# Transforms along w as 64x64 quarters; the second spectral layer by groups of 192 channels

## The chip, the cores and the metric

The kernel runs on one core of a Trainium2 chip. The metric is the device time of one execution in microseconds (us); lower is better. A core has a matrix engine (TensorE, PE in the profile, with PEld for its weight loads), VectorE (DVE), ScalarE (ACT), GpSimd (POOL) and the sync engine (SP), which here only issues transfers. Transfers are issued from SP's and ACT's queues. Matmul results land in PSUM[...] and are copied from there to SBUF by DVE or ACT. Everything is 32-bit floating point.

## The reference

Four layers work on an image of 48 x 48 positions with 768 channels. Layer 0 is a transformer block (attention, then an MLP with gelu), layer 2 a recurrent scan of twelve steps. Layers 1 and 3 are the same spectral block with different weights, and they are what the change is about:

```python
xs = jnp.fft.rfft2(xf32, axes=(1, 2))          # along h and w; 25 frequencies along w
xs = xs.reshape(B, H, Wm, NUM_HEADS, BLOCK)    # 8 blocks of 96 channels
o1r = relu(xr @ w1[0] - xi @ w1[1] + b1[0])    # per block of channels
o1i = relu(xi @ w1[0] + xr @ w1[1] + b1[1])
o2r = o1r @ w2[0] - o1i @ w2[1] + b2[0]
o2i = o1i @ w2[0] + o1r @ w2[1] + b2[1]
out_c = softshrink(o2r) + 1j * softshrink(o2i)
out = jnp.fft.irfft2(out_c, s=(H, W), axes=(1, 2))
return out + x
```

All transforms are matrix products with small constant matrices.

## The kernel before

The stages follow one another: layer 0's projections, attention, the output projection, the MLP, the first spectral layer (names beginning with f1), the scan, the scan's output product (so), and the second spectral layer (f3). A profile line L1529 is line 1529 of the kernel.

A spectral layer has five steps. Forward along w: `spectrum_rows` (L1529) takes a group g of four pairs of image rows and a half of the channels (384). A pair fills 96 partitions, two rows of 48 positions, and one matmul with `fw` of 96 x 112 (both rows' transforms in one matrix, half of it zeros) gives 112 rows of PSUM; ACT and DVE take turns in copying them out (`Evac`), and SP stores the four to `yu` in DRAM. There are 12 such blocks per layer: two halves, six groups. The first layer's run beside the MLP: `afno_follow` gives out one block at a time, `follow` is called between the MLP's matmuls, and its results take the two PSUM buffers of the pool `pt`. The MLP's own products use the pool `pm` with six. The second layer's run beside the scan's output product, whose results `x3` stay in SBUF.

Then `spectrum_mix` goes over items: a half, a group kc of five frequencies, a block b of 96 channels; 2 x 5 x 4 = 40 items. Four stages work on an item: transform along h (`s_fft_h`, L1593), the two layers of the small MLP (`s_mlp1`, L1607 to L1609; `s_mlp2`, L1628 and L1629, then softshrink as `cl` and `Z` on DVE), and the way back along h (`s_ifft_h`, L1643). A step of the loop runs the last stage on item step-4, the third on step-3, the second on step-1, the first on step, then calls `beside(step)`. The finished values of a half and kc (`us`) are stored to `yu` (L1652). In the first layer `us` has the layer's input in the frequency domain added to it (L1646); in the second it is a plain copy by ACT and DVE in turn.

Last comes the way back along w. In the first layer it is `back` in `afno_first` (L1730). In the second it is `back` in `afno_second` (L1826): a block of a half and a group g is four matmuls of 384 columns, each added to `x3` by DVE (L1828), and stored to the output from ACT's queue. The first half's six blocks stand in the mix, at steps 32, 35, 38, 40, 41 and 42; the second half's six come after the mix. The last half's values are reloaded as `gt` in two parts: the rows of the first four kc, and the rest once the last kc has been written.

The order on each engine is that of the code, but a planner may move an instruction ahead of others where its buffers and inputs allow; `tc.keep_in_program_order` pins one to its place. A transfer that reads what another wrote waits on its queue until that one has landed, and what is behind it on the queue waits too.

## Time and profile before

| what | value |
|---|---|
| median of 3 runs | 3606.06 us (3605.91 to 3606.79) |
| the profiled execution's own time | 3605.15 us |
| its span, first to last instruction | 3603.4 us |
| granted clock of TensorE, mean | 0.990 |
| MLP and first layer forward, about | 1850 to 2640 us of the span |
| mix and way back of the first layer, about | 2640 to 2900 us |
| scan | 2900 to 3265 us |
| scan's output product and second layer forward | 3265 to 3366 us |
| mix of the second layer | 3366 to 3571 us |
| end | 3571 to 3603 us |

A group's row names line, engine, operation, then what is written and read, the shapes (for a matmul rows x columns of the array and the moving operand), how often; then busy time, mean ns of one, and idle time of the engine ahead of it with what ended it. An f32 matmul is recorded as two instructions. Their ends are modelled and overlap, so a mean is longer than what one costs.

### The profile page before, as it was taken

The page shows a single profiled execution, that of the slowest core. Times are in us where ns is not written, and L with a number is a line of the kernel's source. Part 1 is how long each engine was busy: PE and PEld are TensorE (multiplying, and loading weights), DVE is VectorE, ACT ScalarE, POOL GpSimd, SP SyncE. Part 2 cuts the span into 40 slices and gives each one's busy share as a digit, 9 for nine tenths or more (in the row PEclk, how much of TensorE's full clock was granted, in tenths as well). Part 3 has the DMA queues.
Part 4 walks back from the last instruction along what each step waited for, and adds up shares of the span by engine and source line. Part 5 has one row for each costly group of instructions (what it writes and reads, how often), then busy time and mean ns, then how long its engine had stood idle before and what let it go on. Part 6 is the DMA issues. An engine that isn't in the chain of part 4 may idle for free. (4 is left out here: it accounts for less than half of the span.)

```text
span 3603.4 us, 52156 instructions
## 1 busy us (share of the span) xinstructions
PE 3539.1 (98%) x20934; PEld 2173.6 (60%) x20934; DVE 2005.8 (56%) x3019; ACT 1140.3 (32%) x1731; POOL 679.0 (19%) x566
## 2 busy tenths in 40 slices
PE   9999999999999999999999999999999998999998
PEld 5666554444444444555555555555578777996685
DVE  7644467776776766564244314233245478995455
ACT  1222245555554545213101210120033365223341
POOL 3212101111111110340000000000023303971131
PEclk9999999999999999999999999999999999999999
DMA  7555556655545443443345334434444303113345
GB/s 267 206 182 184 187 160 182 182 157 147 157 124 148 128 116 86 141 150 114 107 137 175 106 105 141 147 109 125 141 125 111 94 24 103 35 35 98 96 113 158
DMA packets 257371, 477.67 MB, mean 133 GB/s; under 512 B 36030, under 2 KB 209918, under 8 KB 250912
## 3 DMA queue, kind: packets, MB, share of 16 engines
q1 hardware_dynamic: 245600, 452.89, 41.9%
q10 hardware_dynamic: 11520, 21.34, 1.7%
q8 instruction: 168, 2.75, 0.3%
q14 instruction: 83, 0.68, 0.1%
HBM read 330.53 MB, written 143.62 MB: 132 GB/s over the span
## 5 line engine op out<-in xcount | busy, mean ns | idle before, releaser
L669 DVE TENSOR_TENSOR acc<-acc,p 128x928 f32<-128x928 f32 (+1 forms) x480 | 561.0, 1169 | 258.2 <-ACT p L661 216.9
L661 ACT ACTIVATE p<-s 128x928 f32<-128x928 f32 (+1 forms) x540 | 506.8, 940 | 486.8 <-PE s L659 467.9
L649 PE MATMUL s<-qt,kv 64*128 64x464 f32 (+1 forms) x2160 | 520.3, 557 | 5.2 <-DMA qt<-q_d 5.2
L1048 PE MATMUL p<-w,h 128*128 128x384 f32 x1512 | 492.7, 486 | 0.0
L680 PE MATMUL av<-p,kv 128*64 128x464 f32 (+1 forms) x2160 | 442.6, 554 | 0.0
L1048 PEld LDWEIGHTS p<-w,h 128*128 128x128 f32 x1512 | 286.2, 190 | 196.9
L659 PE MATMUL s<-bt,oneh 64*128 64x464 f32 (+1 forms) x1080 | 399.8, 729 | 0.6 <-DMA bt<-rh_d 0.6
L680 PEld LDWEIGHTS av<-p,kv 128*64 128x64 f32 x2160 | 146.9, 137 | 261.2 <-issue 248.4
L649 PEld LDWEIGHTS s<-qt,kv 64*128 64x128 f32 x2160 | 202.9, 187 | 161.5 <-issue 153.4
L985 PE MATMUL p<-x2nT,w 128*128 128x384 f32 x864 | 293.5, 489 | 3.1 <-issue 3.1
L1312 PE MATMUL c<-H,bands 128*48 128x96 f32 x5632 | 244.6, 247 | 10.6 <-issue 8.3
L367 PE MATMUL qk<-xnT,wqk 128*128 128x384 f32 x756 | 249.8, 487 | 0.4 <-DMA wqk<-wqk_d 0.4
L1312 PEld LDWEIGHTS c<-H,bands 128*48 128x48 f32 x5632 | 234.4, 123 | 21.1 <-issue 8.7
L985 PEld LDWEIGHTS p<-x2nT,w 128*128 128x128 f32 x864 | 165.2, 191 | 118.8 <-issue 5.4
L985 PE MATMUL p<-xT,w 128*128 128x384 f32 x648 | 220.8, 486 | 0.0
L1024 POOL TENSOR_TENSOR rr<-rr,ml_b 128x1152 f32<-128x1152 f32 x12 | 33.1, 2759 | 953.5 <-DMA rr<-xr_d 886.6
L980 ACT ACTIVATE h<-h,ml_b 128x384 f32<-128x384 f32 x144 | 88.6, 616 | 345.9 <-DVE h L1000 173.5
L367 PEld LDWEIGHTS qk<-xnT,wqk 128*128 128x128 f32 x756 | 141.4, 190 | 93.4 <-issue 1.0
L1320 POOL TENSOR_TENSOR t<-s,c 128x768 f32<-128x768 f32 x80 | 144.6, 1832 | 180.2 <-DVE s L1283 168.5
L985 PEld LDWEIGHTS p<-xT,w 128*128 128x128 f32 x648 | 123.1, 190 | 85.9
L659 PEld LDWEIGHTS s<-bt,oneh 64*128 64x128 f32 x1080 | 106.7, 187 | 105.0 <-issue 102.9
L172 PE MATMUL v<-wv,xnT 128*128 128x384 f32 x378 | 132.5, 497 | 4.5 <-DVE v_o L181 4.5
(333 smaller groups left out, 4663.5 us busy)
## 6 DMA issues: line engine op xcount, KB each, us to landing
w<-w1s_d SPq DMA_DIRECT2D x36, 768.0 KB, 4.2
w<-w2s_d SPq DMA_DIRECT2D x36, 768.0 KB, 4.3
w<-w1s_d SPq DMA_DIRECT2D x36, 576.0 KB, 3.7
w<-in_mlp_w_dram SPq DMA_DIRECT2D x27, 768.0 KB, 4.5
wqk<-wqk_d SPq DMA_DIRECT2D x12, 1344.0 KB, 10.6
yu<-f_ys SPq DMA_DIRECT2D x24, 672.0 KB, 3.8
f_yt<-yu SPq DMA_DIRECT2D x20, 720.0 KB, 6.7
yu<-f_us SPq DMA_DIRECT2D x18, 720.0 KB, 4.5
```

Of the source, the lines that this page charges most:

```text
L172: nc.tensor.matmul(p[:, :TB], lhsT=rhs[n][:, c, t * P : (t + 1) * P], rhs=w[:, c, :], start=c == 0, stop=c == NC2 - 1)
L367: nc.tensor.matmul(p[:, :TB], lhsT=w[:, n, c, :], rhs=ops[sb][n][:, c, :], start=c == 0, stop=c == NC2 - 1)
L649: nc.tensor.matmul(ps[:, s, :n], lhsT=keys[pr % 2][rows, kt * P : (kt + 1) * P], rhs=held(c)[rows, :n], start=True, stop=False)
L659: nc.tensor.matmul(ps[:, s, :n], lhsT=oneh[rows, b % 2, :], rhs=bts[b // 2][rows, j, :n], start=False, stop=True)
L661: nc.scalar.activation(p, ps[:, :, :n], AF.Exp)
L669: nc.vector.tensor_tensor(probs[c], probs[c], p, ALU.add)
L680: nc.tensor.matmul(avs[c][rows, : size(c)], lhsT=vals[pr % 2][:, kt, rows], rhs=p[:, s, :], start=kt == 0, stop=kt == NT - 1)
L980: nc.scalar.activation(h, h, AF.Gelu, bias=b1c[:, k : k + 1])
L985: nc.tensor.matmul(p[:, :TB], lhsT=w[n][:, c, :], rhs=rhs[n][:, c, :], start=c == 0, stop=c == NC2 - 1)
L1048: nc.tensor.matmul(ps[t][:, :TB], lhsT=hs[left, f][:, t * P : (t + 1) * P], rhs=wt[:, f % KW2, :], start=f == 0, stop=f == NF2 - 1)
L1312: nc.tensor.matmul(ps[r0 : r0 + G, k // 4, cols], lhsT=bands[:, n - GC, i, :] if gr else bands0[:, n, i, :], rhs=H[:, n, :, d : d + NPR], ...
L1320: GP.tensor_tensor(t, sc[:, ch], c1[:, m0 : m0 + GC].unsqueeze(2).to_broadcast([P, GC, RR, NPR]), ALU.mult)
```

## The change

1. *Forward along w.* Image rows of a pair now stand at partitions 0 and 64 (48 used of each 64). A block is two rounds (j) of four matmuls: K = 48 rows from one of the two row halves of the array (a), M = 64 columns into one of the two partition halves of the result (b), 384 columns moving. The two row halves write to different PSUM buffers. Four copies out per block as before, of 128 rows, and two stores. In the MLP these buffers come in turn from `pt` and `pm`.
2. *Layout.* `yu` is now 64 x 48 x 384: a row per frequency and part, a column per image row. `x3` has 112 partitions, the scan's output product writes 112 rows, and its silu works in place.
3. *Second layer's mix.* Four groups of 192 channels in place of two of 384; 4 x 5 x 2 = 40 items. Tiles are loaded two ahead of the one in use, from five buffers. The layer's input is added to `us` in the frequency domain, by DVE, in both layers.
4. *Second layer's way back.* A block is a group of channels and a third c of the image rows: again two rounds of four matmuls (K = 50, M = 64, 384 columns), then a copy by ACT or DVE, and two stores. Three blocks of each of the first three groups stand in the mix at steps 18, 20, 22, 28, 30, 32, 38, 40 and 42. Their reloads are issued right after the group's last write, in three pieces of image rows for each of the two partition halves.
5. *Last group.* Each kc's rows are reloaded as soon as they are written; the last kc is written and reloaded by single blocks of 96 channels. These transfers are pinned to program order. Eight matmuls whose result nobody reads (`keep_warm`) follow the mix, then the group's three blocks, stored from ACT's and SP's queue in turn.

```diff
+def keep_warm(tc, ps, left, right, n):
+    k, m = left.shape
+    for _ in range(n):
+        tc.keep_in_program_order(tc.nc.tensor.matmul(ps[:m, : right.shape[1]], lhsT=left, rhs=right, start=True, stop=True))
 ...
 # mlp_phase
+        places = itertools.cycle(((pt, "t"), (pt, "t"), (pm, "m"), (pm, "m")))
         def psum(name):
-            return pt.tile([P, 512], F32, tag="t", name=name)
+            pool, tag = next(places)
+            return pool.tile([P, 512], F32, tag=tag, name=name)
 ...
 # the scan's output product
-                        t_ = tp.tile([BS, TB], F32, tag="t", name=f"st_{pr}_{half}")
-                        V.tensor_tensor(t_, ps[:BS, :TB], bo[:, cols], ALU.add)
-                        nc.scalar.activation(x3[:, pr, cols], t_, AF.Silu)
+                        V.tensor_tensor(x3[:, pr, cols], ps[:K, :TB], bo[:, cols], ALU.add)
+                        nc.scalar.activation(x3[:, pr, cols], x3[:, pr, cols], AF.Silu)
 ...
 # spectrum_rows
-    ys = pool.tile([YR, 4, TB], F32, tag="ys", name=f"{name}_ys_{half}_{g}", bufs=bufs)
-    for i in range(4):
-        ps = psum(f"f_{half}_{g}_{i}")
-        nc.tensor.matmul(ps[:YR, :TB], lhsT=fw, rhs=x[:, i, :], start=True, stop=True)
-        ev(ys[:, i, :], ps[:YR, :TB])
-    nc.sync.dma_start(yu[half][:, 4 * g : 4 * g + 4, :], ys)
+    ys = pool.tile([P, 2, 2, TB], F32, tag="ys", name=f"{name}_ys_{half}_{g}", bufs=bufs)
+    for j in range(2):
+        ps = [psum(f"f_{half}_{g}_{j}_{a}") for a in range(2)]
+        for a in range(2):
+            keep = slice(a * HD, a * HD + G)
+            for b in range(2):
+                nc.tensor.matmul(ps[a][b * HD : (b + 1) * HD, :TB], lhsT=fw[keep], rhs=x[keep, 2 * j + b, :], start=True, stop=True)
+        for a in range(2):
+            ev(ys[:, j, a, :], ps[a][:, :TB])
+    for b in range(2):
+        nc.sync.dma_start(pairs_of(yu[half], b, g), ys[b * HD : (b + 1) * HD].rearrange("p j a c -> p (j a) c"))
 ...
 # spectrum_mix, s_fft_h and s_ifft_h
+                for ahead in range(3 if groups[group][2] < HB else 1):
+                    at = group * NKC + kc + ahead
+                    if at < len(groups) * NKC:
+                        load(*divmod(at, NKC))
 ...
-            if keep:
-                nc.vector.tensor_tensor(us[:, :, cols], pv, yt[:, :, cols], ALU.add)
-            else:
-                ev(us[:, :, cols], pv)
+            nc.vector.tensor_tensor(us[:, :, cols], pv, yt[:, :, cols], ALU.add)
 ...
 # afno_second
+        def put(group, kc, us, cols):
+            half, b0, _ = groups[group]
+            cs = slice(b0 * BS + cols.start, b0 * BS + cols.stop)
+            pin = tc.keep_in_program_order if group == final else lambda ins: ins
+            pin(nc.sync.dma_start(spectrum_of(yu[half], kc, cs), us[:, :, cols]))
+            if kc == 0:
+                gts[group] = bp.tile([P, G // 2, W], F32, tag="gt", name=f"f3_gt_{group}")
+            if group == final or kc == NKC - 1:
+                rows = slice(2 * KC * kc if group == final else 0, 2 * KC * (kc + 1))
+                step = G // 2 if group == final else 8
+                for r0 in range(0, G // 2, step):
+                    for b in range(2):
+                        pin(nc.sync.dma_start(gts[group][b * HD + rows.start : b * HD + rows.stop, r0 : r0 + step, cols], yu[half][rows, b * (G // 2) + r0 : b * (G // 2) + r0 + step, cs]))
 ...
+        def back(group, c):
+            cols = channels(group)
+            gt = gts[group].rearrange("p (j s) c -> p s j c", s=2)
+            for j in range(2):
+                ps = [psum(f"w_{group}_{c}_{j}_{b}") for b in range(2)]
+                for b in range(2):
+                    keep = slice(b * HD, b * HD + KR)
+                    for s in range(2):
+                        nc.tensor.matmul(ps[b][s * HD : (s + 1) * HD, : 2 * W], lhsT=iw[keep], rhs=gt[keep, s, 4 * c + 2 * j : 4 * c + 2 * j + 2, :], start=True, stop=True)
+                for b in range(2):
+                    ev(x3p[:, b, 4 * c + 2 * j : 4 * c + 2 * j + 2, cols], ps[b][: HD + G, : 2 * W].rearrange("p (j c) -> p j c", j=2))
+                if group == len(groups) - 1:
+                    store((nc.scalar, nc.sync)[j], slice(8 * c + 4 * j, 8 * c + 4 * j + 4), cols)
+            if group < len(groups) - 1:
+                store(nc.scalar, slice(8 * c, 8 * c + 8), cols)
 ...
-        backs = {items - 8: 0, items - 5: 1, items - 2: 2, items: 3, items + 1: 4, items + 2: 5}
+        backs = {each * (q + 1) + 8 + 2 * c: (q, c) for q in range(final) for c in range(3)}
 ...
+        keep_warm(tc, psum("warm"), opened[0][0], opened[0][1][:, :2].rearrange("p n r c -> p (n r c)"), 8)
+        for c in range(3):
+            back(final, c)
```

## The prediction

> **What bounds the kernel now.** I read the page first: TensorE is busy nearly all the span, so a change pays by what it takes from TensorE or from the waits at the end.
>
> ```profile
> span 3603.4 us, 52156 instructions
> ...
> PE 3539.1 (98%) x20934; PEld 2173.6 (60%) x20934; DVE 2005.8 (56%) x3019; ACT 1140.3 (32%) x1731; POOL 679.0 (19%) x566
> ```
>
> Next the groups by line, for the transforms along w: L1529 is the forward one of both spectral layers (f_f the first, so_f the second), L1826 the second layer's way back.
>
> ```profile
> L1826 PE MATMUL f_w<-f_gt,f_iw 100*96 100x384 f32 x96 | 35.2, 522 | 8.6 <-DMA f_gt<-yu 8.6
> L1529 PE MATMUL f_f<-f_x,f_fw 96*112 96x384 f32 x88 | 34.2, 497 | 0.0
> ...
> L1529 PE MATMUL so_f<-x,f_fw 96*112 96x384 f32 x96 | 32.9, 486 | 0.0
> ```
>
> An f32 matmul stands as two records (96 records are 48 matmuls; a few f_f records are missing). The mean is too long for its cost, since records overlap. The chain of work that ended last, in order of time (start, duration), gives the cost: x8, or four matmuls, is 2.58 us, so 0.645 each.
>
> ```profile
> 3362.70 2.58 PE so_f L1529 x8
> ...
> 3571.15 0.67 DVE f_us L66
> 3571.86 4.96 DMA yu<-f_us
> 3576.88 2.67 DMA f_gt<-yu
> 3579.69 18.73 PE f_w L1826 x48
> 3598.44 0.55 DVE x L1828
> ```
>
> The reader is to see the tail: after the last way back along h (3571.1) nothing remains for TensorE until a write and a reload have landed (8.6 us), then half of all ways back along w, 24 matmuls, run at the very end. From 3571.1 to the end at 3603.4 it is 32.2 us. Those 24 should take 15.5 us and take 18.7: the windows (length, then each engine's busy time; PEclk, DMA share and GB/s last) show half clock.
>
> ```profile
> 3577.00:3580.00 3.00, 0.31 (x1) 0.34 (x2) 0.00 (x0) 0.00 (x0) 0.00 (x0) 0.50 0.75 184
> 3580.00:3585.00 5.00, 5.00 (x9) 2.14 (x9) 1.66 (x3) 0.00 (x0) 0.00 (x0) 0.50 0.43 86
> ```
>
> **Price of a block of quarters.** A block (one half, one group of four pairs) is now four matmuls, 2.58 us. It becomes eight, each on 64 rows and 64 columns of the array, in two rounds of four. No row shows four quarters at once. The nearest is attention, where L649 runs two row halves and L680 two column halves; its timeline:
>
> ```profile
> 1199.74 0.94 PE L649 MATMUL s<-qt,kv 64*128 64x464 f32 x4
> 1200.15 0.73 PE L659 MATMUL s<-bt,oneh 64*128 64x464 f32 x2
> 1200.82 2.56 PE L680 MATMUL av<-p,kv 128*64 128x464 f32 x12
> 1203.20 0.95 PE L688 MATMUL rs<-acc,ones 128*64 128x464 f32 x4
> 1203.98 2.51 PE L680 MATMUL av<-p,kv 128*64 128x464 f32 x12
> 1206.42 1.05 PE L649 MATMUL s<-qt,kv 64*128 64x464 f32 x4
> 1206.94 0.73 PE L659 MATMUL s<-bt,oneh 64*128 64x464 f32 x2
> 1207.51 0.94 PE L649 MATMUL s<-qt,kv 64*128 64x464 f32 x4
> 1207.93 0.73 PE L659 MATMUL s<-bt,oneh 64*128 64x464 f32 x2
> ```
>
> The two pairs of L688 take 1203.20 to 1203.98, 0.39 us a pair, which is what one record of 464 columns needs alone (384 columns take 0.645 / 2 = 0.3225); the six of L680 ahead of them take 2.38. So two halves run in the time of one, in rows and in columns. Ends for a block: four at once, 2 x 0.645 = 1.29 us; never more than two, 2.58. The pairs overlap fully both ways, so I take 1.29.
>
> [...] The timeline has one: from L659 to L649, same mode, it is 0.57 (1206.94 to 1207.51), but from L659 to L680 0.67 (1200.15 to 1200.82), +0.10; L680's six rounds take 2.38 for 6 x 0.39, +0.05; on the way back six rounds from 1203.98 end at 1206.31, L649 comes at 1206.42, +0.11, and its first round is 0.52 (1206.42 to 1206.94) instead of 0.42 (1207.51 to 1207.93), +0.10. Out and back costs 0.36 us; I use 0.35. A block is then **1.64 us**. Were the switch free, the result below would be 12.6 us shorter (36 blocks); I take the rows' price.
>
> **The sum, part by part.**
>
> *First layer forward*, 12 blocks, beside the MLP, whose windows show TensorE 250.0 of 250 us busy. Eleven stand as six records, a layer's matmul, then two: 2342.46 to 2344.62 and 2345.27 to 2345.92, 2.81 us, since two PSUM buffers hold it up. The new cycling over two pools gives four. Now 11 x 2.81 + 2.58 = 33.4; then 12 x 1.64 = 19.7. **-13.7**. Two buffers come from the six of the MLP's products: their next product needs a buffer 1.9 us after its last matmul (two more matmuls and one of the next, 3 x 0.645), and the copy out takes 0.56, so nothing waits. Without that cover it would be about 0.6 a block, 7 us.
>
> *Second layer forward*, 12 blocks between the scan's output matmuls, TensorE 100.2 of 101 us: 31.0 to 19.7, **-11.3**. Copies out stay four a block, now of 128 rows; DVE 42 and ACT 42 us in these 101 hide them. The 112-row output matmuls still stream 384 columns, the silu in place moves nothing, and each block has two stores on SP's queue instead of one, 0.4 us issue each: nothing, as SP issues one block per 8 us.
>
> *Mix of the second layer.* 40 items either way, 4.57 us a step, all TensorE (61.0 of 61 us from 3510 on). Before: six blocks inside, 15.5 us. After: nine (three groups by three), 14.8 us. The moved block also issues two copies on DVE and two on ACT (0.56 and 0.48), two stores on ACT's queue (0.32 each, behind which the next item's copies stand), and per group six reloads on SP. DVE takes all 40 additions now (20 moved from ACT at 0.65): cl, Z, two pre, one addition, 2.75 us of a 4.57 us step, so hidden; without room they would cost 13 us. Reloads wait on SP for the last write of their group (4.0 to 5.1 us in the trace); behind them stand only loads that are asked for two tiles, four steps or 18 us, ahead. From the write to the first way back are five steps, 23 us. One step loses its filler: before, a way back stood in each of steps 40, 41 and 42 and covered the DVE chain from f_z to f_u (0.65 + 0.65 and 0.15); step 41 has none now, +1.3 (part of it hides behind copies). Sum -0.7 + 1.3 = **+0.6**.
>
> *Tail.* Only the last group of 192 channels remains: three blocks. But writes and reloads are pinned on SP, so each write waits behind the reload of the one ahead. From the start of item 37's f_u: its write goes at 1.6, lands at 6.1 (4.5); two reloads take 0.75 to issue; item 38's write goes at 6.9 and lands at 10.9 (4.0, the shortest in the trace, as it is a quarter of the size), item 39's at 11.7 and 15.7, the second reload lands 2.7 after issue, 18.8. The last f_u ends at 8.7, so the wait is 10.1 us instead of 8.6: the stall is longer, and what is late is every block of the last group. Then, at full clock, 3.9 us of matmuls, but 1.77 MB of stores: the first leaves 3.1 us after the reload, 6.1 us at 290 GB/s (292 in the window 3590 to 3595), 0.3 and the 1.0 that the program needs after the last landing, 10.5. At half clock: 7.7 of matmuls, 1.0 for copies, 4.4 from the last copy to the end (as now), 13.1.
>
> Which clock? Eight warming matmuls cover 5.2 of the 10.1 us; 4.9 stay idle. The trace halves the clock at 3575.5, 4.4 us after the last matmul. [...] the row alone, 4.4 under 4.9, says half clock. [...] by the row's case 23.2; I take 22.0. 32.2 - 22.0: **-10.2**.
>
> Sum: -13.7 - 11.3 + 0.6 - 10.2 = **-34.6 us**. The profiled execution took 3605.15 us, 1.75 beside its span; so 3570.6, and the median of the runs (3606.06) stands 0.9 above it: **3571.5 us**. The first layer's loads and its way back (two transfers for one, K of 128 for 100, same 96 columns) cost nothing: its mix has TensorE 258.4 of 260 us busy.
>
> **Rivals.** With B for a block, the sum is 36 B - 93.7; it is no gain from B = 2.60 on.
> - *Two at a time* (the slower side): the four quarters issue in order and only two ever overlap, at the 36 blocks. B = 2.58 + 0.35 = 2.93: 11.8 above the time before, 3618 us. For it: no row shows four. Against: rows and columns both pair fully[...].
> - *Staggered*: the row halves follow one phase apart, so a block takes five phases of 0.3225 and the switch, B = 1.96: 11.5 above the forecast, 3583 us. For it: the matmuls of one row half stand ahead of the other's in the code; against: L649's two row halves, written one after the other too, start together.
> - *Switches hidden*: [...] B = 1.35: 10.4 under the forecast, 3561 us. Against: the first rounds at both switches of attention are long.
> - *A new wait in place of the old*: the pinned queue (landings of 5.1, half clock[...]) makes the tail as long as before: 10.2 above the forecast, 3582 us. For it: SP waits three landings in a row; against: half the ways back are gone from it.
>
> **How the numbers follow.** Likeliest 0.54; switches hidden 0.16; staggered 0.16; new wait 0.07; two at a time 0.07. 0.2% of 3606 is 7.2 us, about what this kernel's measurement can tell from no change. Faster: all but the last, 0.93. B between 2.4 and 2.8 would be the same, 0.02; slower 0.05. The range reaches from under the hidden switches (3561, less 3 for a warm tail) to over the staggered case (3583 and 3): 3558 to 3586.
>
> **What would show it.** Four records of L1529's successor starting within some 10 ns, four rounds of 0.32 us a block, and about 0.1 us lost ahead and behind each. MLP and output stages shorter by 14 and 11 us, the mix the same length, the tail 22. Two records at a time would sink the prediction; so would a MLP product waiting for a PSUM buffer, or reloads that reach a way back in the mix late.

## The result, and the profile after

The changed kernel takes 3583.94 us (median of four executions, 3582.01 to 3588.48) where the kernel before takes 3606.43 (four, 3605.91 to 3608.97): a ratio of 0.9945, 95% interval 0.9933 to 0.9957. The gain is 22 us; 34.6 were forecast. On another chip, with unaltered kernels again (n_changed_again below), it was 17 us: 3584.66 and 3601.99, ratio 0.9953 (0.9939 to 0.9967). The profiled execution took 3582.01 us. First the head of its page, and the groups of the transforms along w (L1550 is the forward one, L1891 the second layer's way back).

```profile
span 3580.2 us, 52877 instructions
...
PE 3507.9 (98%) x21238; PEld 2149.6 (60%) x21238; DVE 2002.3 (56%) x3015; ACT 1140.0 (32%) x1735; POOL 679.5 (19%) x566
```

```profile
L1891 PE MATMUL f_w<-f_gt,iw 50*64 50x384 f32 x192 | 20.4, 541 | 12.2 <-DMA f_gt<-yu 12.2
L1550 PE MATMUL so_f<-x,fw 48*64 48x384 f32 x192 | 18.9, 496 | 0.0
```

Twice as many matmuls as before keep TensorE busy for 0.57 to 0.58 of the time (20.4 for 35.2 us, 18.9 for 32.9). Its idle time ahead of the way back, which waits for the reload, has grown from 8.6 to 12.2 us.

By stages, from the first and last matmuls of each in the two traces:

| stage | before, us | after, us | measured | forecast |
|---|---|---|---|---|
| all ahead of the MLP's first matmul | 1608.2 | 1604.6 | -3.6 | 0 |
| MLP with first layer forward | 1016.0 | 1003.0 | -13.0 | -13.7 |
| first layer's mix and way back, scan | 643.3 | 644.1 | +0.9 | 0 |
| scan's output product with second layer forward | 94.8 | 85.2 | -9.6 | -11.3 |
| from there to the mix | 4.2 | 4.3 | +0.1 | 0 |
| mix, first f_x to the end of the last f_u | 204.7 | 207.9 | +3.2 | +0.6 |
| tail, from there to the end | 32.2 | 31.0 | -1.2 | -10.2 |

The first row is code that the change does not touch. In the runs below, which are alike up to the first f_x of the first spectral layer, that f_x starts between 2609.0 and 2617.1 us; so the 3.6 us of the first row are within that spread and are not counted for the change: without them the profiled executions are 19.5 us apart, not 23.1. The time of a single execution does not show a difference of 4 us. I therefore give for each run the time from that f_x to the end too, and the two parts of the tail.

What is missing is mostly in the tail. The chain that ended last in the changed kernel (start, duration, what):

```profile
3547.36 0.65 DVE f_Z L1672
3548.40 0.55 DVE x L66
3549.02 3.73 DMA out_dram<-x
3552.82 5.36 DMA yu<-f_us
3558.98 4.06 DMA yu<-f_us
3563.11 3.33 DMA f_gt<-yu
3566.53 4.77 PE f_w L1891 x26
```

Here a store to the output is a link of the chain ahead of a write to `yu` that reads other data and writes another tensor. The waits of SP's queue between 3539 and 3563 us (line, what it waited for, us in total, times, longest):

```profile
SPq L1877 <- DMA yu<-f_us: 12.4, 3, 5.2
SPq L1869 <- DMA out_dram<-x: 7.4, 2, 6.3
```

L1877 are the reloads, which wait for the write they read; that was reckoned with. L1869 are the writes, and two of them waited, 7.4 us together, for stores of the way back. SP's timeline and DVE's show when each went (DVE's L1684 makes the values that are written):

```profile
3540.34 0.70 SPq L1877 DMA_DIRECT2D f_gt<-yu  x2
3547.45 0.31 SPq L1869 DMA_DIRECT2D yu<-f_us  x1
3550.40 1.24 SPq L1877 DMA_DIRECT2D f_gt<-yu  x2
3552.82 0.45 SPq L1869 DMA_DIRECT2D yu<-f_us  x1
3558.19 0.69 SPq L1877 DMA_DIRECT2D f_gt<-yu  x2
3558.98 0.31 SPq L1869 DMA_DIRECT2D yu<-f_us  x1
```

```profile
3540.80 0.65 DVE L1684 TENSOR_TENSOR f_us<-f_u,f_yt 96x480 f32<-96x480 f32 x1
...
3546.68 0.65 DVE L1670 TENSOR_SCALAR f_cl<-f_z 96x480 f32<-96x480 f32 x1 [2.84 <-PE f_z L1667]
3547.36 0.65 DVE L1672 TENSOR_TENSOR f_Z<-f_z,f_cl 96x480 f32<-96x480 f32 x1
3547.94 1.01 DVE L66 COPY x<-f_w 112x384 f32<-112x384 f32 x2
3548.87 1.21 DVE L1684 TENSOR_TENSOR f_us<-f_u,f_yt 96x480 f32<-96x480 f32 x2
```

Item 37's values are ready at 3541.45, its write goes at 3547.45. The addition of item 38, whose f_u ended at 3544.9, comes only at 3548.87, behind item 39's softshrink and two copies: the planner put it there, and the two halves of the last kc are ready within 0.6 us of each other. After that, the windows (length, busy time of PE, PEld, DVE, ACT and POOL; clock, DMA share, GB/s):

```profile
3558.20:3563.00 4.80, 0.00 (x0) 0.00 (x0) 0.00 (x0) 0.00 (x0) 0.00 (x0) 0.50 0.54 77
3563.00:3566.50 3.50, 0.00 (x0) 0.00 (x1) 0.00 (x0) 0.00 (x0) 0.00 (x0) 0.50 0.30 53
3566.50:3571.00 4.50, 4.47 (x26) 2.24 (x30) 1.11 (x2) 0.53 (x2) 0.00 (x0) 0.50 0.14 28
```

TensorE stands still, and the last matmuls begin at half clock (0.50).

### The profile page after: what moved, and what is told of

Read it like the earlier page. It is cut to its first block, busy times and chain, and to the rows that moved or that the text cites. A ratio compares the mean times of both kernels' runs of the same rounds, so it can differ in the third digit from the quotient of the medians.

```text
span 3580.2 us, 52877 instructions
## 1 busy us (share of the span) xinstructions
PE 3507.9 (98%) x21238; PEld 2149.6 (60%) x21238; DVE 2002.3 (56%) x3015; ACT 1140.0 (32%) x1735; POOL 679.5 (19%) x566
## 4 chain that ended last, share of the span: by engine, by line
PE 90%; DVE 3%; DMA 3%; POOL 2%; ACT 1%; issue 1%; SPq 0%; ACTq 0%; POOLq 0%; DVEq 0%
PE p L996 14%; PE p L1059 13%; PE s L657 12%; PE av L688 12%; PE qk L375 6%; PE c L1223 4%; PE s L667 3%; PE c L1323 3%; PE v L180 3%; PE pj L180 2%; PE f_z L1666 2%; PE f_z L1667 2%; PE f_x L1631 2%; PE so L1410 2%; PE f_u L1682 2%; PE f_o L1645 1%
## 5 line engine op out<-in xcount | busy, mean ns | idle before, releaser
L1666 PE MATMUL f_z<-f_w,f_o 97*96 97x96 f32 x800 | 134.2, 249 | 0.0
```

The lines of the kernel that those rows point to most:

```text
L1666: nc.tensor.matmul(out, lhsT=o1[:, j, 1:3, :].rearrange("c r h -> c (r h)"), rhs=w2t[:, b, 0, :], start=True, stop=False)
```

## Experiments

All are edits of the changed kernel. The last three columns are of one execution, the profiled one: from the first f_x of the first spectral layer to the end; from the end of the last f_u to the first f_w of the last group (the stall); and from the end of the last f_u to the end (the tail). The runs a to d were on one chip, e to h on a second, k to n on a third, o to r on a fourth, s and t on the second again; medians of different chips are not told apart where their ranges overlap.

| run | time, us (range) | f_x to end | stall | tail |
|---|---|---|---|---|
| before | 3606.43 (3605.91 to 3608.97) | 977.7 | 8.6 | 32.2 |
| changed | 3583.94 (3582.01 to 3588.48) | 970.3 | 17.4 | 31.0 |
| n_changed_again | 3584.66 (3584.48 to 3591.07) | 970.7 | 16.0 | 30.2 |
| a_stores_held | 3582.39 (3578.96 to 3586.76) | 964.3 | 10.4 | 23.7 |
| o_pool_stores | 3582.07 (3579.52 to 3584.29) | 967.7 | 13.6 | 28.5 |
| e_nopin | 3579.83 (one) | 968.7 | 10.3 | 24.3 |
| b_one_piece | 3583.75 (3580.40 to 3585.07) | 969.1 | 14.7 | 29.3 |
| c_writes_first | 3582.83 (3579.22 to 3586.07) | 968.3 | 13.8 | 28.8 |
| t_add | 3582.97 (3581.34 to 3584.49) | 967.8 | 13.9 | 28.3 |
| d_warm24 | 3583.28 (3581.30 to 3587.61) | 970.1 | 17.2 | 30.3 |
| f_mixwarm | 3584.61 (3580.61 to 3587.72) | 970.5 | 16.5 | 30.0 |
| k_all_wfirst | 3580.90 (3576.37 to 3584.62) | 966.0 | 11.4 | 27.1 |
| l_all_one | 3578.76 (3577.77 to 3581.99) | 964.8 | 10.8 | 25.8 |
| m_all_nopin | 3579.04 (3577.32 to 3580.54) | 963.2 | 11.3 | 24.7 |
| p_pool_one | 3577.77 (3573.81 to 3585.30) | 965.8 | 12.5 | 26.6 |
| q_pool_wfirst | 3580.26 (3579.74 to 3581.69) | 966.0 | 12.8 | 26.7 |
| r_pool_nopin | 3580.30 (3577.84 to 3585.89) | 963.4 | 13.0 | 26.0 |
| s_chain | 3579.08 (3578.46 to 3580.76) | 964.3 | 11.1 | 25.6 |

### The stores of the mix

```diff
# a_stores_held: steps 40 and 42 copy, but do not store
+        held = ((final - 1, 1), (final - 1, 2))
 ...
-            if group < len(groups) - 1:
+            if group < len(groups) - 1 and (group, c) not in held:
                 store(nc.scalar, slice(8 * c, 8 * c + 8), cols)
 ...
+        for group, c in held:                       # behind the warming, pinned on SP
+            store(nc.sync, slice(8 * c, 8 * c + 8), channels(group))
         for c in range(3):
             back(final, c)
```

> The stores of the last two ways back in the mix (steps 40 and 42) are issued on SP behind the last group's reloads instead of on ACT ahead of them. Theory (the last group's writes stand on SP behind those stores[...]): item 37's write goes within 2 us of the start of its f_u instead of 7.7, item 38's some 4 us later, so the first f_w comes about 7 us sooner after the last f_u (about 10 us instead of 17.5), and the time falls by 4 to 7 us, since 1.2 MB of stores now leave at the end. Rival (the landings of the three writes and reloads alone make the stall; the stores do not hold them): item 37's write goes at 7.7 us as before, the stall stays at 17 us, and the time is the same or up to 4 us longer.

The stall fell to 10.4 us and the tail to 23.7, 1.7 more than the forecast's 22.0. Item 37's write went 1.8 us after the start of its f_u, and SP's waits for a store were gone:

```profile
SPq L1878 <- DMA yu<-f_us: 18.8, 4, 7.5
SPq L1870 <- DVE f_us L1684: 4.7, 2, 3.4
```

The stall answers as the theory said; the medians differ by 1.5 us only, and the ranges overlap. In the profiled execution the mix was 1.6 us longer (its last step fell under half clock, see below) and all ahead of the first f_x 7 us longer, which the edit does not touch. This run takes away two things at once: the wait, and the stores' bytes. The next keeps the bytes.

```diff
# o_pool_stores: the same stores at the same moment, from GpSimd's queue
-                store(nc.scalar, slice(8 * c, 8 * c + 8), cols)
+                store(nc.gpsimd if group == final - 1 and c else nc.scalar, slice(8 * c, 8 * c + 8), cols)
```

> The stores of steps 40 and 42 are issued at the same moments as in the changed kernel, but from GpSimd's queue instead of ACT's. The same bytes move at the same time. Theory (the write is held because it shares a completion counter with a store of the queues that ACT and SP use[...]): item 37's write goes 1.6 to 2 us after the start of its f_u instead of 7.7, and the stall from the last f_u to the first f_w falls from 17.4 to 10 to 12 us. Rival (the memory is full of the stores' bytes, and the write could not have gone or landed sooner in any case): the write goes sooner, but lands at the old moment, or it goes 7 us late as before; the stall stays at 15 us or more.

SP's timeline, and its part of the chain:

```profile
3541.51 0.31 SPq L1869 DMA_DIRECT2D yu<-f_us  x1
3547.47 0.70 SPq L1877 DMA_DIRECT2D f_gt<-yu  x2
3549.57 0.31 SPq L1869 DMA_DIRECT2D yu<-f_us  x1
```

```profile
3549.57 5.00 DMA yu<-f_us
...
3555.37 3.87 DMA yu<-f_us
3559.26 3.28 DMA f_gt<-yu
```

The write went at 3541.5, 1.8 us after the start of its f_u (3539.7), but took 6.0 us to land; in the changed kernel it went 6 us later and took 3.0. Both theories have a part. With the queue alone the stall falls by 3.8 us, from 17.4 to 13.6. What the bytes add has to be read from executions with a like last step: in a_stores_held it took 6.1 us instead of 4.3, which gave the early writes more time before the last f_u. n_changed_again had such a step too, and a stall of 16.0; from there to 10.4 it is 5.6 us, so the bytes' part is about 1.8. Three pairs below that differ in holding the stores or moving them to GpSimd's queue (and in the number of warming matmuls) give 1.4 to 1.7: k and q, l and p, m and r.

That the wait is for a shared completion counter is in the changed kernel's trace: a transfer names the semaphore that its landing raises, and the transfers of SP and ACT together name eight (101, 102, 104 to 108, 110). At 3547.40 an instruction on SP waits for semaphore 102; the write behind it, at 3547.45, names 102 too, and the last transfer ahead of it that did so is a store of step 40, issued at 3540.73, 6.7 us earlier. In o_pool_stores no write waited for a store: what SP waited for ahead of the writes was DVE, 2.3 us in all.

```diff
# e_nopin
-            pin = tc.keep_in_program_order if group == final else lambda ins: ins
+            pin = lambda ins: ins
```

> The last group's transfers are no longer pinned to program order, and the planner is free to move them on SP: it places the two writes of the last kc next to each other and the reloads in fours behind the writes. Theory (the pinned order, in which a write waits for the landing of the write before it and for that one's reloads, makes up part of the stall): the two last writes go together, as where only the reload between them is left out, and the stall after the last f_u is 13 to 14 us instead of 17.4. Rival (without pins a reload of early rows lands in front of a write and delays it): stall 17 us or longer.

The stall was 10.3 us, below what the theory asked, but not by its mechanism. In the planner's order item 37's write went at 3541.5, 1.8 us after the start of its f_u, so no store held it. The two last writes did not go together: item 39's went 3.6 us behind item 38's, after a wait of 3.2 us for a store of step 42.

```profile
3552.57 4.03 DMA out_dram<-x
...
3556.67 2.54 DMA yu<-f_us
```

So waits for stores decided here too. A part of the short stall is the clock: the last step of the mix took 7.8 us instead of 4.3, so more of the landings lay inside the mix, and the mix became 4.7 us longer. How much the pins cost by themselves stays open.

### Fewer landings in a row

```diff
# b_one_piece: the last kc is written and reloaded once
-            last = kc == NKC - 1 and group == len(groups) - 1
+            last = kc == NKC - 1 and group == len(groups) - 1 and n == HB
```

> The last kc is written and reloaded once, 192 channels wide (runs of 768 bytes), instead of in two pieces of 96. Theory of a chain of landings (each of the two writes takes 4 to 5.4 us to land, and both stand in a row): one landing and one reload issue leave the chain, the stall after the last f_u falls from 17.5 to about 10 us, the time by 6 to 8 us. Rival (the stall is set by the landing of the stores ahead alone, up to 3552.8 in the trace, and the write that comes after it): the write goes at 3552.8, lands in 3 to 4 us and the reload in 3.3, so the stall is 10.5 us as well, but item 37's write still goes 7.7 us after its f_u. If neither holds, and the pieces hide each other, the stall stays at 17 us or grows by the wider piece's longer landing.

```diff
# c_writes_first: two writes, then one reload of both
+            if group == final and kc == NKC - 1:
+                if cols.start == 0:
+                    return
+                cols = slice(0, W)
+                cs = slice(b0 * BS, b0 * BS + W)
             if group == final or kc == NKC - 1:
```

> The last kc is still written in two pieces of 96 channels, but nothing is reloaded between them; one reload of 192 channels follows the second. Theory of the queue (item 39's write waits on SP behind item 38's reload, which waits for item 38's landing, 5.4 us): the two writes go within 1 us of each other at about 3553, the second lands at about 3558.5, the reload at 3562; the stall falls from 17.5 to 13 us, the time by 4 us. Rival ([...] two writes at once take as long as two in a row): the second lands at about 3562 and the stall stays at 16 to 17 us.

They took 2.7 and 3.6 us from the stall: c nearly what the queue's theory had, b little over a third of what the landings' had. In each a write still waited for stores (8.6 us in two waits in c; in b the last write went at 3555.7, as a store landed). And neither reached its gain at the end: the second reload of 192 channels landed 6.4 us after its issue in c, 6.8 in b, where one of 96 took 3.3, so the 24 matmuls started and stopped (from first to last 8.7 us in c and 8.3 in b, not 6.2).

### The late addition, and the whole chain in order

t_add pins item 38's addition ahead of item 39's softshrink and the copies of step 42, on top of o_pool_stores.

```diff
# t_add
+        def in_order(i):
+            return tc.keep_in_program_order if name == "f3" and i >= len(items) - 1 else lambda ins: ins
 ...
-            nc.vector.tensor_tensor(us[:, :, cols], pv, yt[:, :, cols], ALU.add)
+            in_order(i + 1)(nc.vector.tensor_tensor(us[:, :, cols], pv, yt[:, :, cols], ALU.add))
 # and in_order(i) around cl and Z; the copies of step 42 pinned too
```

> As with the stores of steps 40 and 42 on GpSimd's queue, and item 38's addition stands on DVE ahead of item 39's two softshrink instructions and of two copies of the way back, as in the code; in the changed kernel the planner put it behind them, at 3548.9, 4 us after its f_u had ended, so that item 38's values were ready only 0.6 us before item 39's. Theory (that addition, not SP, then holds item 38's write): the write no longer waits for it and goes right behind item 37's reload, at 8.5 us after the start of item 37's f_u instead of 9.8, so 1.3 us sooner; the stall after the last f_u falls from 13.6 to 12.2 us. Rival (SP's row of landings is the bound, and the write lands no sooner, since it meets the stores of step 40 still moving): stall 13 to 14 us as before.

The rival held. The write went 9.0 us after the start of item 37's f_u (9.8 without the edit), but took 6.3 us to land instead of 5.0: stall 13.9 us. In both runs the stores of step 42 moved beside it; why it took longer here is not shown. The late addition cost nothing while landings stood in a row.

```diff
# s_chain: t_add, and (warm(n) is keep_warm with n matmuls)
+            if group == final and kc == NKC - 2:
+                return
+            if group == final and kc == NKC - 1:
+                if cols.start == 0:
+                    kc = NKC - 2          # item 37's reload behind item 38's write
+                cols = slice(0, W)
+                cs = slice(b0 * BS, b0 * BS + W)
 ...
+            if step == 41:
+                warm(2)
-        keep_warm(..., 8)
+        warm(14)
```

> The same addition early, the same stores on GpSimd's queue, and the writes of items 37 and 38 both ahead of item 37's reload, one reload of 192 channels behind item 39's write; two warming matmuls in step 41 and 14 after the mix. Theory: the writes go 1.7, 5.8 and 10.4 us after the start of item 37's f_u, each as soon as its values are there; the last one lands 4 us on, the reload 4.7 us behind it: 9 to 10 us from the last f_u to the first f_w, and at full clock 22 to 23 us to the end, as the prediction had it; the time 7 to 9 us under the changed kernel. Rival (the stores' bytes make every landing 5 to 6 us, whatever the order): 12 us or more to the first f_w and 26 us to the end, as in the versions with one piece or both writes first.

The writes went 1.8, 5.9 and 10.2 us after, as wanted; the stall of 11.1 us lies between the theories, the tail of 25.6 at the rival's 26. The last write took 5.5 us to land and the wide reload 6.4 (end of the chain):

```profile
3551.68 5.47 DMA yu<-f_us
...
3557.49 6.36 DMA f_gt<-yu
```

### Everything together

k, l and m hold the stores (as a), put two warming matmuls into step 41 and 14 after the mix, and write the last kc as c, as b, or as e. p, q and r have the stores on GpSimd's queue (as o) instead, with two warming matmuls in step 41 too and 19, 19 and 17 after the mix, and write it as b, c and e. n is the changed kernel itself beside k, l and m.

> The changed kernel once more, unaltered, beside the next three on the same chip, as the measure for them: 3584 us, a stall of 17 us between the last f_u and the first f_w, 31 us from the last f_u to the end.

> Three edits together: the stores of the ways back of steps 40 and 42 held until the last group's reloads are issued, no reload between the two last writes, and warming matmuls (two in step 41, where TensorE idles 1.4 us, and 14 instead of 8 after the mix). Theory (the tail is made of the wait for those stores, of landings in a row and of the clock): from the last f_u to the first f_w 9 to 10 us, the last 24 matmuls in 3.9 to 4.2 us at full clock, from the last f_u to the end 19 to 21 us instead of 31, the mix not longer than 208 us; the time 10 us under the unaltered changed kernel. Rival (once nothing waits, the 2.9 MB of stores at the end are the bound: 10 us at 290 GB/s from the last reload on): 23 us or more, as with the stores held alone, and a time 7 to 8 us under.

> The same with the last kc written and reloaded in one piece of 192 channels. Theory (fewer transfers in the row are worth more than an early start of half of them): the write goes 1.1 us after the start of the last f_u's copy, lands in 3 to 5.4, the reload in 3.3 to 5: 9 to 11 us from the last f_u to the first f_w, 20 to 22 us to the end. Rival (one transfer alone takes longer to land than two halves side by side, as 5.4 against 4.0 us in the two runs with one edit): 1 to 2 us longer than with two writes.

> The same stores held and the same warming matmuls, with the two writes and their reloads in separate pieces and not pinned. Theory (with the stores held, nothing on SP waits for anything but the last group's own landings, so that pins or no pins make no difference beyond the reload between the writes): within 2 us of the version with both writes first. Rival (without pins the planner moves a reload ahead of a write): 2 us or more longer.

> Those stores from GpSimd's queue, the last kc in one piece of 192 channels, two warming matmuls in step 41 and 19 after the mix (12.3 us, as both reloads had landed about 12 us after the last f_u in the version with held stores). Theory: stall 10 to 12 us until the first f_w, the 24 matmuls in 4 to 5 us at full clock, and only the last group's 1.8 MB of stores left at the end: 21 to 22 us from the last f_u to the end, the time 9 us under the changed kernel. Rival (contention only moves: what the stores no longer take at the end they take from the write and the reload): 25 us or more, as with held stores.

> The same with both writes of the last kc first and one reload behind them. Theory: as with one piece, within 1.5 us either way (with held stores the two stood at 27.1 and 25.8 us from the last f_u to the end). Rival (two writes at once gain more where no store holds them): 2 us or more shorter than one piece.

> The same with two writes and two pairs of reloads, not pinned, and 17 warming matmuls (with held stores the matmuls could start 11.3 us after the last f_u and ran without a break). Theory: 20 to 22 us from the last f_u to the end; the time 9 us under the changed kernel. Rival: contention with the stores lengthens the landings and it stays at 24 us or more.

On one chip l (3577.77 to 3581.99) and m (3577.32 to 3580.54) lie wholly under the changed kernel (3584.48 to 3591.07): 5.6 to 5.9 us by the medians, about half of what the theory asked; k is 3.8 us under it, with ranges that touch. So l and m beat both kernels (m's ratio to the kernel before is 0.9932, 0.9919 to 0.9946). p's ratio is the same (0.9918 to 0.9946), but its chip has no run of the changed kernel to set it against. None of the six reached a tail of 22 us: 24.7 to 27.1, which is the rival's 23 and more. One piece and both writes first came out alike from GpSimd's queue, as forecast (26.6 and 26.7). The two that reload in pieces have the shortest tail of their three (m 24.7, r 26.0): their last 24 matmuls run without a break, 6.0 us from first to last against 7.0 to 8.5 where the last reload is wide. They are also the shortest from the first f_x, 963.2 and 963.4, but m owes 1.2 us of that to a mix with less half clock (see below), and r 1.7 us to stages ahead of that mix, which the edits do not touch.

### The clock

```diff
# d_warm24
-        keep_warm(..., 8)
+        keep_warm(..., 24)
```

> 24 warming matmuls instead of 8 after the mix. They take 15.5 us at full clock, so they end about 2 us before the first f_w of after (3566.5). Theory (half clock costs the end 2.3 us in the last 24 matmuls and some 1 us more in copies that follow them): the granted clock is 1.00 in the last stage, the last f_w matmuls take 3.9 instead of 6.2 us, the time falls by 2 to 3 us. Rival (the end is bound by the stores' bandwidth): the matmuls are faster, the time the same within 1 us.

A miss: warming ended 1.6 us ahead of the first f_w, and the clock fell all the same, to 0.50 for 3.41 us. The windows (the third number from the end is the granted clock):

```profile
3564.35:3567.76 3.41, 1.74 (x13) 0.58 (x16) 0.00 (x0) 0.48 (x1) 0.00 (x0) 1.00 0.25 48
3567.76:3571.17 3.41, 3.41 (x28) 1.51 (x24) 1.67 (x3) 0.86 (x2) 0.00 (x0) 0.50 0.41 102
```

In e_nopin the same happened in the middle of the mix. Step 41 has the idle time that the prediction had named, 1.5 us here; it cost more than itself:

```profile
3540.63:3544.04 3.41, 1.88 (x22) 1.75 (x20) 1.96 (x3) 0.00 (x0) 0.04 (x1) 1.00 0.70 137
3544.04:3551.77 7.73, 7.73 (x38) 4.56 (x38) 1.86 (x3) 0.48 (x1) 0.00 (x0) 0.50 0.77 144
```

Of the twelve profiled executions without warming in step 41, five lengthen the last step of the mix from 4.3 us to between 5.9 and 7.8; of the seven with it, none does. The clock's changes lie on a grid: in the traces of the kernel before and of the changed one they (19 and 17) all stand whole multiples of 3.41 us apart. I laid windows of 3.41 us over each trace, with the changes of the clock as borders. In the five executions that lost the clock the gap lay inside one window, in which TensorE was busy for 1.88 to 1.99 us. In six of the seven others a border cut 0.02 to 0.2 us off the gap (2.01 to 2.18 us busy in the window with the rest; in the changed kernel a gap of 1.43 us, 0.11 cut off, 2.10 busy). One does not fit: b_one_piece kept the clock, though its gap ended 0.08 us ahead of a border; so what makes the clock fall is not shown. First the window of n_changed_again, which lost the clock, then that of b_one_piece:

```profile
3544.96:3548.38 3.42, 1.99 (x16) 1.34 (x15) 1.31 (x2) 0.00 (x0) 0.00 (x0) 1.00 1.04 165
```

```profile
3543.05:3546.47 3.42, 1.99 (x22) 1.78 (x20) 2.06 (x4) 0.00 (x0) 0.09 (x1) 1.00 0.71 106
```

```diff
# f_mixwarm (warm(n) is keep_warm with n matmuls)
+            if step in (0, 1):
+                warm(2)
+        warm(3)
```

> Warming matmuls in the gaps at the start of the second layer's mix: three ahead of it, two in each of the steps 0 and 1 (3.9 us at full clock). Theory (TensorE idles there 1.8, 1.4 and 1.4 us, the granted clock falls to half for 13.65 us where it was 6.83 us before the change, and that made the mix 3.2 us longer): with the gaps filled the half clock at the start goes or stays at most 3.4 us, and the time from the first f_x to the end of the last f_u falls from 207.9 to 201 to 204 us. Rival (the mix is longer for another reason, its ways back or reloads): the half clock goes, but the mix keeps 207 us, since the warming matmuls take the place of what they save.

The half clock at the start of the mix came down from 13.65 to 3.41 us. The mix took 206.6 us, of which 1.6 are its last step under half clock; without that 205.0, 2.9 less than in the changed kernel. The wait ahead of it grew by 2.6 us, from 4.3 to 7.0. So the remedy gives nothing; 206.6 is what the rival named, and even 205.0 misses the theory's 201 to 204. The cause shows better in executions that differ by chance: from the first f_x to the start of item 38's f_u it is 202.3 to 202.9 us in the fourteen with 13.65 us at half clock at the start, 201.5 in the three with 10.24 (a, m, n), and 203.4 in h_pair, below, with 17.07. The changed kernel, then m_all_nopin:

```profile
3342.39:3356.04 13.65, 10.84 (x48) 9.20 (x49) 1.69 (x5) 4.13 (x9) 3.63 (x5) 0.50 0.22 54
```

```profile
3348.27:3358.51 10.24, 7.97 (x30) 6.33 (x31) 1.43 (x4) 2.56 (x8) 2.15 (x3) 0.50 0.23 59
```

That is 0.7 to 1.2 us for 3.41 us of half clock.

### The price of a block of quarters

```diff
# g_double: in spectrum_rows, second layer, each round once more
+        if name == "f3":
+            for a in range(2):
+                keep = slice(a * HD, a * HD + G)
+                for b in range(2):
+                    nc.tensor.matmul(ps[a][b * HD : (b + 1) * HD, :TB], lhsT=fw[keep], rhs=x[keep, 2 * j + b, :], start=True, stop=True)
# h_pair: two blocks at a time
-            if n and n % 2 == 0:
+            if n and n % 4 == 0:
+                rows_in(n // 2 - 2, scan_psum)
                 rows_in(n // 2 - 1, scan_psum)
 ...
+                rows_in(2 * NTB - 2, scan_psum)
                 rows_in(2 * NTB - 1, scan_psum)
```

> In the second layer's 12 forward blocks every round of four quarters is issued twice into the same banks. Theory (four quarters run at once, 0.3225 us a round, f32 in four records; the rest of a block's 1.64 us is the change of the array's mode): each block grows by 1.29 us, the time between the first and the last output matmul (11 blocks) by 14.2 us, from 85.4 to 99.6. Rival (two at a time, or one row half a phase later): 2.58 or 1.61 us a block, 113.8 or 103.1 us.

> The second layer's forward blocks are issued two by two, so that half of the changes between the array's modes go; nothing else changes. Theory (a change out and back costs 0.35 us, ahead of and behind a block): 5 of the 11 blocks between the first and the last output matmul lose their change, and this stage falls from 85.4 to about 83.6 us. Rival (the change of mode costs nothing by itself, and the 0.35 us are the filling and draining of every round of four): the stage stays at 85.4 us, but for a block that leaves it at the end (then 83.8 with a longer time from there to the mix).

One execution each: 3597.2 and 3580.7 us. g: 99.5 us between the first and the last output matmul, for 99.6 by the theory. Its chain (L1550 is a round, L1555 the same round once more):

```profile
3338.20 0.81 PE so_f L1550 x8
3339.01 0.65 PE so_f L1555 x8
3339.65 0.65 PE so_f L1550 x8
3340.30 0.65 PE so_f L1555 x8
3340.94 5.34 PE so L1410 x16
```

x8 are the records of four matmuls: one round of four quarters, 0.65 us, where one f32 matmul over 96 rows and 112 columns took 0.645 before. Four run at once.

h: 82.3 us, below both numbers, because a whole block more moved behind the last output matmul, which the theory's 83.6 had left out: 85.2 less 1.64 for it and 5 x 0.35 are 81.8. The rival had named this case, with 83.8; so a change has a price, 0.27 us by the stage as a whole (six changes and one block's 1.29 us make the 2.9 us that went). The price shows best in the chains; first the changed kernel's, then h's:

```profile
3319.61 1.45 PE so_f L1550 x16
3321.06 5.34 PE so L1410 x16
```

```profile
3311.77 10.50 PE so L1410 x32
3322.28 2.74 PE so_f L1550 x32
```

Two blocks and sixteen output matmuls take 2 x (1.45 + 5.34) = 13.58 us in the one and 10.50 + 2.74 = 13.24 in the other: 0.34 us for one change out and back.

## Why the prediction was right and where it failed

- **Price of a block** (1.29 + 0.35): right. Records start four at a time, within 20 ns, and a round takes 0.65 us for f32, not the sum of two. Four run at once, and a change of the tiles' form costs time: out and back 0.34 us by h_pair's chain, for 0.35 from attention's rows, where L649 has 64*128 and L680 128*64. The staggered rival would give the same total as was measured (3583 us), but not g_double's 99.5 us, for which it asked 103.1.
- **First layer forward**: -13.0 for -13.7 (by its own terms 11 x 2.81 + 2.58 - 19.7, which is 13.8). **Second**: -9.6 for -11.3; 11 of its 12 blocks lie between the marks, 11 x 0.94 = 10.3. Of the other 0.7 us some 0.5 are the clock: a stretch at half clock reached 1.7 us into the output matmuls where it reached 0.7 before.
- **Mix**: the step that lost its filler idles 1.43 us, as forecast 1.3. The +3.2 for +0.6 are mostly the clock: 13.65 us at half clock at the start for 6.83 before; at 0.7 to 1.2 us for each 3.41 that makes 1.4 to 2.4 of the 2.6 us in excess. I had priced the mix at full clock throughout. Why half clock lasted longer there than before stays open.
- **Tail**: this is the step that failed, 31.0 us for 22.0. Of the 9.0 us, 7.3 are the wait between the last f_u and the first f_w (17.4 for 10.1); the other 1.7 lie behind it, where the last matmuls ran at half clock (13.6 us from the first f_w to the end, for its 13.1 at half clock and 10.5 at full). The 22.0, between 10.1 + 10.5 and 10.1 + 13.1, was an estimate of mine. "From the start of item 37's f_u: its write goes at 1.6": it went at 7.7. "Item 38's write goes at 6.9": at 13.0. "Item 39's at 11.7": at 19.2. The order of the landings was right, and each had been named; what was left out is that SP's writes also wait for stores that ACT's queue had issued. The prediction priced these stores as 0.32 us of issue on ACT each and asked only what stands behind them on ACT. With them out of the way the stall is 10.4 us (11.4, 10.8 and 11.3 in k, l and m, whose last step kept its clock), for 10.1 in the prediction, and the tail 23.7 for 22.0. A second term was mis-sized: I took the shortest landing, 4.0 us, "as it is a quarter of the size"; with the stores on the way the small writes took 3.8 to 6.3 (o_pool_stores, t_add). A third, that the write of item 38 could go once its f_u was done, left out its addition on DVE, 4 us late; it had no price of its own (t_add).
- **Which rival**: what came is "a new wait in place of the old", at 3582 us, to which I gave 0.07. Its numbers were near for what happened after the wait (landings of 5.4 and 4.1 us for its 5.1, and half clock); its mechanism, three landings in a row on SP, was a part only. That the measured time lies inside the stated range, 3558 to 3586, is luck: the upper end was set by the staggered case, which did not come.

## What to carry to other kernels

When a transfer is put on a critical queue, list the transfers of the other queues in the last few microseconds too: here a write on SP's queue waited up to 6.3 us for a store of ACT's to land, which had other data. Give small writes at a time when other stores move the landing time of a busy moment (3.8 to 6.3 us here), not the shortest of the trace (4.0). Where a stage has short idle gaps, look for half clock after each (it came in five of twelve executions here), and fill gaps inside a step (then in none of seven) rather than ahead of the stage, where filling took the place of what it saved: in f_mixwarm the wait ahead of the mix grew by 2.6 us.

## What the runs showed of the hardware

- In the changed kernel transfers of SP and ACT shared eight completion counters (semaphores 101, 102, 104 to 108, 110), and a write waited up to 6.3 us for an unrelated store; in c_writes_first two waits of writes for stores made 8.6 us. With the stores of steps 40 and 42 on GpSimd's queue (o_pool_stores) no write waited for a store.
- TensorE's clock was halved at the end of a window of 3.41 us in which it had been busy for 1.74 us (d_warm24), 1.88 (e_nopin) or 1.99 (n_changed_again); the half-clock stretches from the first spectral layer on that did not run into the end were 3.41, 6.83, 10.24, 13.65 or 17.07 us. One gap of 1.4 to 1.5 us was enough in the five executions above, where it lay inside one window, and did nothing in seven others, though in one of these (b_one_piece, 1.99 us busy) it lay inside a window too.
- A reload of 192 channels into twice ten partitions took 6.4 us in s_chain and c_writes_first, where little else moved (500 of 506 packets and all 498 were of its queue), and 6.8 in b_one_piece; one of 96 channels took 3.3 in the changed kernel and in o_pool_stores. In two stretches of c_writes_first, during the reload, the DMA share was 0.63 and 0.74, at 73 and 86 GB/s:

```profile
3560.50:3562.40 1.90, 0.00 (x1) 0.03 (x1) 0.00 (x0) 0.00 (x0) 0.00 (x0) 0.50 0.63 73
3559.60:3561.60 2.00, 0.00 (x0) 0.00 (x0) 0.00 (x0) 0.00 (x0) 0.00 (x0) 0.50 0.74 86
```
